# Attention weights transposed on VectorE and moved by DMA between partition quarters, in place of TensorE transposes

## The chip, the cores and the metric

The kernel runs on one core of a Trainium2 chip. The metric is the device time of one execution in microseconds (us). The engines are named as the profile names them: PE (matrix multiplication, with PEld for its weight loads), DVE (vector), ACT (scalar and activation), POOL, and SP, which here only issues DMAs. Each engine works through its own queue of instructions in order, and they meet through semaphores.

## The reference

A batch of 8 matrices x of 512 x 512 (f32) passes four stages, each as `x = x + layernorm(stage(layernorm(x)))`:

```
attention 0:  scores = x^T x;  softmax;  context = weights . x
ffn 0:        x . (sum of 8 factors) / sqrt(8) + bias
attention 1:  RMS norm, 8 query heads and 2 key/value heads of 64,
              softmax(q k^T / 8) v, output projection, + x
ffn 1:        silu(x gate^T * gs) * (x up^T * us), then down^T * ds
```

The change is in attention 1. For each of 8 heads and 512 rows there is a softmax row of 512 weights, and the product with the values needs those weights transposed: the key position must lie on the partitions.

## The kernel before

The whole program is recorded first and ordered afterwards. Class `Recorder` (line 54) takes operations by `add` with an engine, an assumed duration and the buffers that they read and write; `issue` (line 116) then lays them out with a list scheduler: on each engine it takes, among the operations that could start within the engine's `SLACK` of the first, the one with the earliest due time. Due times come from `due` (line 1351) and the tables `DUE` and `SHIFT`; `change` (line 60) is an assumed price of switching the matrix array's shape. The result is a fixed order for each engine in which operations of several batch elements are interleaved. Buffers come from pools: 8 tiles "big" of 128 x 2048, 4 tiles "e" of 128 x 512, 5 and 3 PSUM banks "f" and "g". All loads but the gate, up and down weights are issued on SP, in the order of the list, as are the stores of the output; those weights are loaded from POOL.

`stage_attn1` (line 767) computes for each batch element the transposed normalized input hT, keys kT, values v, and queries qT for four pairs of heads (the two heads of a pair sit in partitions 0-63 and 64-127 and use different key/value heads). `attend(i, u)` (line 934) is the unit of work: head pair i, row half u (256 rows), so 8 units per batch element and 64 in all. For each of its two blocks s of 128 rows:

- line 944 computes the scores of both heads into two PSUM banks;
- `softmax_row` (line 567), for each head: DVE takes the negated maximum (573), ACT the exponential with its sum (580), DVE the reciprocal (590) and DVE scales the row (597);
- line 975 transposes the scaled rows on PE, 16 pieces of 64 x 128, into two PSUM banks;
- line 987 copies them on ACT, two copies, into aT, a tile "big".

Then `values_of` (line 1006) multiplies values with aT, eight matmuls for the unit, and line 1019 copies the result over the queries in qT. `project` (line 1027) is the output projection. For the last batch element (`EARLY`) the units are ordered by row half, and ffn 1 begins on the first half; the other elements go by head pair.

At the first batch element the kernel also sums the factors (line 419) and checks the weights' low bits (line 463), both with DVE work. `layers` is written twice: the second copy runs only if that check fails, and doesn't run here; counts below are of the copy that runs.

Of the kernel before, what the change touches and what calls it, by code (L numbers as in the profile page):

```python
# [17 lines left out]
P = 128  # L18
# [35 lines left out]
class Recorder:  # L54
# [4 lines left out]
    @staticmethod  # L59
    def change(eng, old, new):  # L60


        if new is None or new == old:
            return 0.0
        if eng == "ACT":
            return 1.3
        return 0.09 * (old is None or old.strip("r") != new.strip("r")) + 0.12 * new.endswith("r")

    def __init__(self):
        self.ops = []  # L70
# [178 lines left out]
def layers(  # L249
# [28 lines left out]
    G = 2  # L278
# [285 lines left out]
    def mm(bank, us, go, reads, room=(), state="128x128"):  # L564
        return add("PE", us, go, reads=reads, writes=[bank], room=room, state=state)

    def softmax_row(sc, e):

        nmax, tot, rtot = Buf("s1"), Buf("s1"), Buf("s1")
        add(  # L570
            "DVE",
            0.68,
            lambda: nc.vector.tensor_reduce(nmax.t[:, :], sc.t[:, :], AX.X, ALU.max, negate=True),  # L573
            reads=[sc],
            writes=[nmax],
        )
        add(
            "ACT",
            0.88,
            lambda: nc.scalar.activation(  # L580
                e.t[:, :], sc.t[:, :], AF.Exp, bias=nmax.t[:, :], accum_out=tot.t[:, :]
            ),
            reads=[sc, nmax],
            writes=[e, tot],
            state="exp",
        )
        add(
            "DVE",
            0.16,
            lambda: nc.vector.reciprocal(rtot.t[:, :], tot.t[:, :]),  # L590
            reads=[tot],
            writes=[rtot],
        )
        add(
            "DVE",
            0.48,
            lambda: nc.vector.tensor_scalar(e.t[:, :], e.t[:, :], rtot.t[:, :], None, ALU.mult),  # L597
            reads=[rtot],
            writes=[e],
        )  # L600

    def transpose_to(dst, src, copy="ACT", room=()):

# [20 lines left out]
    def transpose_two(b, t, srcs, room=(), copy=True):  # L624

        pts = [Buf("f") for _ in range(2)]

        def go():  # L630
            for j, r in enumerate(srcs):
                for c in range(KT):
                    for hf in range(2):
                        hp = ts(hf, DH)
                        nc.tensor.transpose(  # L635
                            pts[hf].t[:, :].rearrange("p (j c q) -> p j c q", j=2, c=KT)[:, j, c, :],
                            ap(r)[hp, ts(c, P)],
                            ident[hp, hp],
                        )

        add(
            "PE",
            0.56,
            go,
            reads=[ref(r) for r in srcs],
            writes=pts,
            room=[b, *room],
            state="64x128",
        )

        def into(hf):
            return lambda tt: tt[:, :, t * P : (t + 2) * P].rearrange(
                "p c (j h q) -> p h j c q", j=2, h=2
            )[:, hf, :, :, :]

        def bank(hf):
            return pts[hf].t[:, :].rearrange("p (j c q) -> p j c q", j=2, c=KT)

        if copy:
            for hf in range(2):  # L660

                def go(hf=hf):
                    nc.scalar.copy(into(hf)(b.t), bank(hf))

                add("ACT", 0.6, go, reads=[pts[hf]], writes=[(b, (t, hf)), (b, (t + 1, hf))])
        return pts, into, bank

    def column(b, t):

# [97 lines left out]
    def stage_attn1(x, b):  # L767
# [163 lines left out]

        def attend(i, u):
            aT = Buf("big")
            for s in (2 * u, 2 * u + 1):
                when(kinds[0], b, i, u, s % 2)
                es = [Buf("e") for _ in range(G)]
                scs = [Buf("f") for _ in range(G)]

                def scores(i=i, s=s, scs=scs):
                    for g in range(G):
                        gp = ts(g, DH)
                        nc.tensor.matmul(  # L944
                            scs[g].t[:, :],
                            qT.t[gp, i, ts(s, P)],
                            kT.t[gp, :],
                            start=True,
                            stop=True,
                        )  # L950

                add(
                    "PE",
                    0.87,
                    scores,
                    reads=[(qT, (i, u)), kT],
                    writes=scs,
                    room=[*es, aT],
                    state="64x128",
                )  # L960
                for g in range(G):
                    softmax_row(scs[g], es[g])


                pts = [Buf("f") for _ in range(2)]

                def halves(b):
                    return b.t[:, :].rearrange("p (c q) -> p c q", q=DH)

                def transposes(es=es, pts=pts):  # L970
                    for g in range(G):
                        for t in range(NT):
                            for hf in range(2):
                                hp = ts(hf, DH)
                                nc.tensor.transpose(  # L975
                                    halves(pts[hf])[:, g * NT + t, :],
                                    es[g].t[hp, ts(t, P)],
                                    ident[hp, hp],
                                )

                add("PE", 0.56, transposes, reads=es, writes=pts, room=[aT], state="64x128")
                for hf in range(2):

                    def place(hf=hf, s=s, aT=aT, pts=pts):
                        lo = s % 2 * P + hf * DH
                        copy = nc.scalar.copy
                        copy(columns_of(aT)[:, :, lo : lo + DH], halves(pts[hf]))  # L987

                    add(
                        "ACT",  # L990
                        0.6,
                        place,
                        reads=[pts[hf]],
                        writes=[(aT, 2 * s + hf)],
                    )
            when(kinds[1], b, i, u)
            po = Buf("f")

            def columns_of(b):
                return flat(b.t).rearrange("p (c q) -> p c q", q=2 * P)  # L1000

            def values_of(aT=aT, po=po):
                for t in range(NT):
                    for g in range(G):
                        gp = ts(g, DH)
                        nc.tensor.matmul(  # L1006
                            po.t[gp, : 2 * P],
                            v.t[:, t * P + g * DH : t * P + (g + 1) * DH],
                            columns_of(aT)[:, g * NT + t, :],
                            start=(t == 0),  # L1010
                            stop=(t == NT - 1),
                        )
# [4 lines left out]
                "ACT",  # L1017
                0.4,
                lambda i=i, u=u, po=po: nc.scalar.copy(
                    qT.t[:, i, ts(u, 2 * P)], po.t[:, : 2 * P]  # L1020
                ),
                reads=[po],
                writes=[(qT, (i, u))],
# [264 lines left out]


DUE = {  # L1290
    "x": (-2.595,),
    "fsum": (0.4631, 0.0036),
    "scales": (-1.7557,),
    "wd": (0.2919,),
    "low": (0.8154, 1.1722),
    "a0.norm": (0.602,),
    "a0.row": (-0.0133, 0.0064),
    "a0.out": (0.6155, 0.0012),
    "f0": (-0.2291, 0.103),
    "a1.norm": (0.498, -0.0333),  # L1300
    "a1.kv": (-2.1194,),
    "a1.q": (0.5487, 0.0684),
    "a1.row": (0.5193, 0.0805, 0.0215, -0.0006),
    "a1.mix": (1.3287, 0.0052, 0.0124),
    "a1.out": (1.6207, -0.0361),
    "e1.row": (0.4681, -0.0113, 0.0525, -0.0529),
    "e1.mix": (-2.4837, 58.3341, 0.0746),
    "e1.out": (1.1439, 0.155, 0.0456),
    "f1.norm": (-0.1878, 0.009),
    "f1.gate": (1.5586, 0.0013),  # L1310
    "f1.down": (1.7415, 0.1322, 0.0313),
    "h1.norm": (1.5393, -1.0876, 0.0495),
    "h1.gate": (2.1757, 0.4491, 4.54),
    "h1.down": (1.6071, -1.5421, 1.3412),
}

SHIFT = {
    ("a0", 0): 0.0119,
    ("a1", 0): -0.3641,
    ("f0", 0): 0.0009,  # L1320
    ("f1", 0): -0.1337,
    ("x", 0): 0.0116,
    ("a0", 1): 0.0009,
    ("a1", 1): -0.1282,
    ("f0", 1): -0.3583,
    ("f1", 1): -0.001,
    ("x", 1): 0.0094,
    ("a0", 2): 0.0721,
    ("f1", 2): -0.0021,
    ("x", 2): 0.3533,  # L1330
    ("a1", -2): -0.0219,
    ("f0", -2): -0.0106,
    ("f1", -2): -0.0418,
    ("x", -2): -0.0328,
    ("a0", -1): 0.0045,
    ("a1", -1): -0.1019,
    ("f0", -1): 0.0436,
    ("f1", -1): 0.0947,
}

STAY = {"PE": 0.1755}

SLACK = {"PE": 0.123, "ACT": 0.0985, "DVE": 0.0676, "POOL": 0.7848, "SP": 0.1357}

SMALL = 0.8265
FSUM_POOL = (0, 3)
EARLY = (-1,)
FEW = 4
# [54 lines left out]
```

## Time and profile before

| | |
|---|---|
| median of 3 runs | 1516.56 us (1516.08 to 1517.06) |
| the profiled execution: its own time | 1518.21 us |
| the profiled execution: span from first to last instruction | 1516.3 us |
| granted PE clock | 0.996 |
| DMA traffic | 108.04 MB |
| SP queue (q1): bytes, share of 16 engines | 55.34 MB, 11.5% |

A row of the list of groups reads: line, engine, operation, output <- inputs, shapes, count | busy us, mean ns of one | idle time before, and what ended it. Instructions on PE overlap, so count times mean exceeds busy. An f32 matmul appears as two records, an f32r matmul or a transpose as one. A row of the timeline reads: start, duration, engine, line, and how many like instructions were merged (x16). In a table by stages the columns are the stretch, its length, busy us and count of PE, PEld, DVE, ACT and POOL, the granted clock, the share of the DMA engines and GB/s.

Some rows that the text needs, from the groups with their shapes kept apart:

```profile
L944 PE MATMUL f<-kv,big 64*128 64x512 f32 x512 | 131.2, 613 | 0.1
...
L1099 ACT CAST hl<-hd 128x768 fp32r<-128x768 f32 x32 | 26.7, 836 | 26.0 <-PE g L1233 25.8
...
L1099 ACT CAST hl<-hd 128x640 fp32r<-128x640 f32 x32 | 23.3, 729 | 16.5 <-PE g L1233 9.9 <-DVE hd L1204 6.4
```

### The profile page before, as it was taken

What the parts mean: (1) busy time and instruction counts of PE and PEld (TensorE: products, weight loads), DVE (VectorE), ACT (ScalarE), POOL (GpSimd) and SP (SyncE); (2) the same over time, 40 slices, a digit from 0 to 9 for tenths busy, and PEclk for the clock granted to TensorE, in tenths of its full rate; (3) what the DMA queues carried; (4) which work ended last, traced back from release to release, by engine and by line L of the source; (5) the groups of instructions that cost most, each with busy time, mean ns of one, the idle gap of its engine ahead of it and who ended that gap; (6) DMA issues with size and microseconds to landing.
All of it is one profiled execution on the core that took longest, in us unless ns stands there. A gap on an engine that the chain in (4) does not pass through costs nothing.

```text
span 1516.3 us, 23151 instructions
## 1 busy us (share of the span) xinstructions
PE 1472.7 (97%) x8562; PEld 909.2 (60%) x8562; DVE 1052.4 (69%) x2227; ACT 671.1 (44%) x1426; POOL 578.6 (38%) x884
## 2 busy tenths in 40 slices
PE   5999999999999999999999999999999999999997
PEld 3444557655766557665566656665566655666575
DVE  6899865768558685586846868466774757748745
ACT  3226645642276414663256622565325642266312
POOL 6661142236412374033721347103571116602341
PEclk9999999999999999999999999999999999999999
DMA  9523046112521214212151122411233103420281
GB/s 335 158 84 112 2 105 112 36 42 49 98 63 43 48 44 91 56 48 65 29 104 36 57 56 49 97 37 43 56 70 84 36 15 77 77 63 22 56 161 38
DMA packets 156698, 108.04 MB, mean 71 GB/s; under 512 B 7072, under 2 KB 137120, under 8 KB 156576
## 3 DMA queue, kind: packets, MB, share of 16 engines
q0 software_dynamic: 98736, 51.13, 17.9%
q1 hardware_dynamic: 57840, 55.34, 11.5%
q8 instruction: 70, 1.15, 0.3%
q14 instruction: 52, 0.43, 0.1%
HBM read 98.06 MB, written 8.39 MB: 70 GB/s over the span
## 4 chain that ended last, share of the span: by engine, by line
PE 80%; DVE 9%; POOL 6%; DMA 2%; issue 2%; SPq 0%; ACT 0%; POOLq 0%; DVEq 0%; ACTq 0%
PE g L1165 18%; PE g L1233 11%; PE f L944 7%; PE f L1006 7%; PE f L915 7%; PE f L1032 6%; PE f L724 6%; PE f L975 5%; PE f L693 4%; PE f L746 3%; PE f L635 2%; POOL rstd L532 2%; PE f L896 2%; PE f L885 2%; DVE row L540 1%
## 5 line engine op out<-in xcount | busy, mean ns | idle before, releaser
L1165 PE MATMUL g<-hl,wgu 128*128 128x512 f32 (+1 forms) x1408 | 339.3, 394 | 1.9 <-DMA wgu<-in_gate_t 1.7
L1165 PEld LDWEIGHTS g<-hl,wgu 128*128 128x128 f32 x1408 | 256.7, 189 | 71.9 <-DVE s L573 10.6
L525 POOL TENSOR_SCALAR ve<-mv 128x1 f32<-128x1 f32 x224 | 62.5, 280 | 591.6 <-DVE mv L521 584.4
L573 DVE TENSOR_REDUCE s<-f 128x1 f32<-128x512 f32 x288 | 184.9, 684 | 107.3 <-PE f L944 66.5
L580 ACT ACTIVATE e<-f,s 128x512 f32<-128x512 f32 x288 | 195.9, 688 | 76.5 <-DVE s L573 73.3
L559 POOL TENSOR_TENSOR x<-x,z 128x512 f32<-128x512 f32 x120 | 163.8, 1368 | 48.2 <-DVE z L540 42.7
L1233 PE MATMUL g<-wd,hl 128*128 128x512 f32 x704 | 174.8, 401 | 1.4 <-DVE hl L1108 1.4
L987 ACT COPY big<-f 128x512 f32<-128x512 f32 x256 | 135.9, 593 | 71.8 <-PE f L975 71.5
L1233 PEld LDWEIGHTS g<-wd,hl 128*128 128x128 f32 x704 | 129.4, 188 | 52.3 <-issue 20.7
L597 DVE TENSOR_SCALAR e<-e,s 128x512 f32<-128x512 f32 x288 | 145.3, 508 | 8.4
L532 POOL TENSOR_TENSOR rstd<-ve,mhalf 128x1 f32<-128x1 f32 x224 | 142.0, 638 | 16.0
L387 POOL DMA_DIRECT2D wgu<-in_up_t x92 | 75.0, 815 | 151.1 <-PE g L1165 146.6
L944 PE MATMUL f<-kv,big 64*128 64x512 f32 x512 | 131.2, 613 | 0.1
L1195 DVE SCALAR_TENSOR_TENSOR sig<-g,gs,sig 128x512 f32<-128x512 f32 x84 | 62.7, 747 | 87.4 <-ACT sig L1185 87.1
L1006 PE MATMUL f<-big,kv 128*64 128x256 f32 x1024 | 122.6, 384 | 0.0
L1032 PE MATMUL f<-ws,big 128*128 128x512 f32 x256 | 116.6, 600 | 0.7 <-ACT big L870 0.7
L746 PE MATMUL f<-fsum,rT 128*128 128x512 f32 x256 | 115.7, 595 | 0.2
L915 PE MATMUL f<-big,ws 128*128 128x512 f32 x256 | 115.5, 599 | 0.0
L724 PE MATMUL f<-big,big 128*128 128x512 f32 x256 | 114.8, 597 | 0.0
L1185 ACT ACTIVATE sig<-g,gs 128x512 f32<-128x512 f32 x84 | 58.6, 698 | 119.4 <-PE g L1165 99.6
L387 POOL DMA_DIRECT2D wgu<-in_gate_t x92 | 72.6, 790 | 99.9 <-PE g L1165 93.3
L1204 DVE SCALAR_TENSOR_TENSOR hd<-g,us,sig 128x512 f32<-128x512 f32 x84 | 62.8, 747 | 67.0 <-PE g L1165 63.8
(91 smaller groups left out, 1920.2 us busy)
## 6 DMA issues: line engine op xcount, KB each, us to landing
wgu<-in_gate_t POOLq DMA_DIRECT2D x92, 256.0 KB, 3.3
wgu<-in_up_t POOLq DMA_DIRECT2D x92, 256.0 KB, 3.3
x<-in_x SPq DMA_DIRECT2D x32, 256.0 KB, 2.6
ws<-in_wq_t SPq DMA_DIRECT2D x32, 256.0 KB, 3.3
ws<-in_wo_t SPq DMA_DIRECT2D x32, 256.0 KB, 2.6
out<-x SPq DMA_DIRECT2D x32, 256.0 KB, 2.0
hd<-in_factors SPq DMA_DIRECT2D x28, 256.0 KB, 5.3
wd<-in_down_t POOLq DMA_DIRECT2D x11, 256.0 KB, 8.4
```

The lines of the kernel that those rows point to most:

```text
L532: lambda: nc.gpsimd.tensor_tensor(rstd.t[:, :], ve.t[:, :], mhalf, ALU.pow),
L559: lambda: on.tensor_tensor(ap(xt), ap(xt), y.t[:, :], ALU.add),
L573: lambda: nc.vector.tensor_reduce(nmax.t[:, :], sc.t[:, :], AX.X, ALU.max, negate=True),
L580: lambda: nc.scalar.activation(e.t[:, :], sc.t[:, :], AF.Exp, bias=nmax.t[:, :], accum_out=tot.t[:, :]),
L724: nc.tensor.matmul(po.t[:, :], xnT.t[:, j, ts(t, P)], wT.t[:, j, :], start=(j == 0), stop=(j == KT - 1),)
L746: nc.tensor.matmul(po.t[:, :], xnT.t[:, kt, :], fsum.t[:, kt, :], start=(kt == 0), stop=(kt == KT - 1),)
L915: nc.tensor.matmul(pq.t[:, :], wq.t[:, kt, :], hT.t[:, kt, :], start=(kt == 0), stop=(kt == KT - 1),)
L944: nc.tensor.matmul(scs[g].t[:, :], qT.t[gp, i, ts(s, P)], kT.t[gp, :], start=True, stop=True,)
L1006: nc.tensor.matmul(po.t[gp, : 2 * P], v.t[:, t * P + g * DH : t * P + (g + 1) * DH], columns_of(aT)[:, g * NT + t, :], start=(t == 0), sto ...
L1032: nc.tensor.matmul(po.t[:, :], qT.t[:, i, ts(t, P)], flat(wos[i].t), start=(i == 0), stop=(i == NPAIR - 1),)
L1165: nc.tensor.matmul(bank.t[:, cut], w.t[:, kt, :], d.t[:, kt, cut], start=(n == 0), stop=(n == KT * len(xs) - 1),)
L1233: nc.tensor.matmul(po.t[:, :], ap(o)[:, it - lo, :], wd.t[:, it, :], start=(it == 0 and k == 0), stop=(it == NI - 1 and k == len(ops) - 1),)
```

## The change

In attention 1 the transposes on PE and the copies from PSUM are gone. In their place, for each of the four softmax rows-by-heads of a unit, ACT scales the row by the reciprocal, and DVE transposes it in 32 x 32 blocks into a second tile "big", tb (`small_blocks`). When all four are there, SP issues 16 DMAs of 32 partitions x 512 elements (64 KB) from tb to aT (`to_quarters`): source quarter i goes, in four parts, to the four destination quarters a. The columns of aT come to lie in another order, so the product with the values reads them as four runs of 64, and the copy to qT puts the results back in order. Attention 0 keeps its transposes on PE and its scaling on DVE. The tables of due times, `SHIFT`, `STAY`, `SLACK` and `SMALL` are replaced throughout, and so is the order of instructions on every engine, in all stages.

```diff
-        return 0.09 * (old is None or old.strip("r") != new.strip("r")) + 0.12 * new.endswith("r")
+        if old is not None and old.strip("r") == new.strip("r"):
+            return 0.0
+        return 0.21 if new.endswith("r") else 0.09
...
-    def softmax_row(sc, e):
+    def softmax_row(sc, e, on="DVE"):
...
+        if on == "ACT":
+            add(
+                "ACT",
+                0.6,
+                lambda: nc.scalar.mul(e.t[:, :], e.t[:, :], rtot.t[:, :]),
+                reads=[rtot],
+                writes=[e],
+            )
+        else:
...
+    def small_blocks(dst, n, groups, src, us=0.62):
+        def go():
+            d = flat(dst.t).rearrange(
+                "p (a g k s c) -> p a g k s c", a=4, g=groups, k=KT, c=32
+            )[:, :, n % groups, :, n // groups, :]
+            nc.vector.transpose(d, ap(src).rearrange("p (k a c) -> p a k c", k=KT, a=4))
+
+        add("DVE", us, go, reads=[ref(src)], writes=[(dst, n)])
+
+    def to_quarters(dst, src, us=6.0):
+        def go():
+            for i in range(4):
+                for a in range(4):
+                    nc.sync.dma_start(
+                        flat(dst.t)[ts(a, 32), ts(i, D)], flat(src.t)[ts(i, 32), ts(a, D)]
+                    )
+
+        add("SP", us, go, reads=[src], writes=[dst], lat=2.2)
...
         def attend(i, u):
-            aT = Buf("big")
+            aT, tb = Buf("big"), Buf("big")
...
-                    room=[*es, aT],
+                    room=[*es, tb],
                     state="64x128",
                 )
                 for g in range(G):
-                    softmax_row(scs[g], es[g])
...
-                add("PE", 0.56, transposes, reads=es, writes=pts, room=[aT], state="64x128")
-                for hf in range(2):
...
-                        copy(columns_of(aT)[:, :, lo : lo + DH], halves(pts[hf]))
...
+                    softmax_row(scs[g], es[g], "ACT")
+                    small_blocks(tb, s % 2 * G + g, G, whole(es[g]))
+            to_quarters(aT, tb)
...
-                return flat(b.t).rearrange("p (c q) -> p c q", q=2 * P)
+                return flat(b.t).rearrange("p (i c q) -> p c i q", i=4, q=2 * 32)
...
-                            po.t[gp, : 2 * P],
+                            po.t[gp, : 2 * P].rearrange("p (i q) -> p i q", i=4),
                             v.t[:, t * P + g * DH : t * P + (g + 1) * DH],
-                            columns_of(aT)[:, g * NT + t, :],
+                            columns_of(aT)[:, g * NT + t, :, :],
...
-                    qT.t[:, i, ts(u, 2 * P)], po.t[:, : 2 * P]
+                    qT.t[:, i, ts(u, 2 * P)].rearrange("p (s i c) -> p i s c", s=2, i=4),
+                    po.t[:, : 2 * P].rearrange("p (i s c) -> p i s c", s=2, i=4),
...
-    "a1.row": (0.5193, 0.0805, 0.0215, -0.0006),
-    "a1.mix": (1.3287, 0.0052, 0.0124),
+    "a1.row": (0.6822, 0.0734, 0.1964, -0.0076),
+    "a1.mix": (1.4015, 0.1652, 0.0008),
...
-STAY = {"PE": 0.1755}
-
-SLACK = {"PE": 0.123, "ACT": 0.0985, "DVE": 0.0676, "POOL": 0.7848, "SP": 0.1357}
-
-SMALL = 0.8265
+STAY = {"PE": 0.3655}
+
+SLACK = {"PE": 0.4719, "ACT": 0.3146, "DVE": 0.1972, "POOL": 0.4366, "SP": 0.1357}
+
+SMALL = 1.6694
```

More of the change, by code (lines that the diff above doesn't have):

```diff
@@ L593, in softmax_row @@
         )
[L594 to L600, printed above, removed]
+        if on == "ACT":
[7 more added lines that the diff above has]
+        else:
+            add(
+                "DVE",
+                0.48,
+                lambda: nc.vector.tensor_scalar(e.t[:, :], e.t[:, :], rtot.t[:, :], None, ALU.mult),
+                reads=[rtot],
+                writes=[e],
+            )
     def transpose_to(dst, src, copy="ACT", room=()):
@@ L666, in transpose_two @@
         return pts, into, bank
+    def small_blocks(dst, n, groups, src, us=0.62):
[11 more added lines that the diff above has]
+                        flat(dst.t)[ts(a, 32), ts(i, D)], flat(src.t)[ts(i, 32), ts(a, D)]
+                    )
+        add("SP", us, go, reads=[src], writes=[dst], lat=2.2)
     def column(b, t):
@@ L961, in attend @@
                 for g in range(G):
-                    softmax_row(scs[g], es[g])
[L965 to L972, printed above, removed]
-                            for hf in range(2):
[L974 to L979, printed above, removed]
-                add("PE", 0.56, transposes, reads=es, writes=pts, room=[aT], state="64x128")
[L982 to L995, printed above, removed]
+                    softmax_row(scs[g], es[g], "ACT")
+                    small_blocks(tb, s % 2 * G + g, G, whole(es[g]))
+            to_quarters(aT, tb)
             when(kinds[1], b, i, u)
@@ L1290 @@
 DUE = {
[L1291 to L1302, printed above, removed]
-    "a1.row": (0.5193, 0.0805, 0.0215, -0.0006),
-    "a1.mix": (1.3287, 0.0052, 0.0124),
-    "a1.out": (1.6207, -0.0361),
-    "e1.row": (0.4681, -0.0113, 0.0525, -0.0529),
@@ L1307 @@
[L1307 to L1314, printed above, removed]
+    "x": (-4.5218,),
+    "fsum": (-0.547, 0.014),
+    "scales": (-1.2959,),
+    "wd": (-0.7415,),
+    "low": (1.8698, 0.1987),
+    "a0.norm": (0.0158,),
+    "a0.row": (-0.0659, -0.763),
@@ new lines @@
+    "a0.out": (0.9091, -0.0574),
+    "f0": (-0.3562, 0.1296),
+    "a1.norm": (-0.3362, 0.1194),
+    "a1.kv": (-1.2134,),
+    "a1.q": (0.5561, 0.1876),
+    "a1.row": (0.6822, 0.0734, 0.1964, -0.0076),
+    "a1.mix": (1.4015, 0.1652, 0.0008),
+    "a1.out": (2.1241, -0.0582),
+    "e1.row": (0.1817, 0.0337, 0.8262, -0.0122),
+    "e1.mix": (-3.788, 317450.7115, 0.0865),
+    "e1.out": (2.4047, 0.0474, -0.0519),
+    "f1.norm": (-0.6898, 0.8102),
+    "f1.gate": (1.1806, 0.0018),
+    "f1.down": (1.9561, 0.2922, 0.0028),
@@ L1315 @@
+    "h1.norm": (1.4106, -0.7397, 1.6211),
+    "h1.gate": (3.3436, 0.0244, 0.1058),
+    "h1.down": (0.7682, -266.647, 0.0299),
 }
 SHIFT = {
[L1318 to L1338, printed above, removed]
-}
-STAY = {"PE": 0.1755}
-SLACK = {"PE": 0.123, "ACT": 0.0985, "DVE": 0.0676, "POOL": 0.7848, "SP": 0.1357}
-SMALL = 0.8265
+    ("a0", 0): -0.1698,
+    ("a1", 0): -0.2727,
+    ("f0", 0): -0.235,
+    ("f1", 0): 0.2207,
+    ("x", 0): 0.5279,
+    ("a0", 1): 0.1932,
+    ("f0", 1): 0.2686,
+    ("x", 1): 0.1051,
+    ("a0", 2): 0.1267,
+    ("a1", 2): -0.1561,
@@ L1346 @@
+    ("f1", 2): -0.003,
+    ("x", 2): 0.0002,
+    ("a0", -2): 0.0203,
+    ("f0", -2): 0.0665,
+    ("f1", -2): 0.0816,
+    ("x", -2): 0.1179,
+    ("a0", -1): 0.5856,
+    ("a1", -1): -0.4355,
+    ("f0", -1): -0.3224,
+    ("f1", -1): -0.0373,
+}
+STAY = {"PE": 0.3655}
+SLACK = {"PE": 0.4719, "ACT": 0.3146, "DVE": 0.1972, "POOL": 0.4366, "SP": 0.1357}
+SMALL = 1.6694
 FSUM_POOL = (0, 3)
```

## The prediction

> **What bounds the kernel now.** I read the page's busy times first, then its chain, then the groups of PE with their shapes kept apart.
>
> ```profile
> PE 1472.7 (97%) x8562; PEld 909.2 (60%) x8562; DVE 1052.4 (69%) x2227; ACT 671.1 (44%) x1426; POOL 578.6 (38%) x884
> ...
> PE 80%; DVE 9%; POOL 6%; DMA 2%; issue 2%; SPq 0%; ACT 0%; POOLq 0%; DVEq 0%; ACTq 0%
> ```
>
> ```profile
> L1006 PE MATMUL f<-big,kv 128*64 128x256 f32 x1024 | 122.6, 384 | 0.0
> ...
> L975 PE MATMUL f<-ident,e 64*128 64x64 f32 x2048 | 88.0, 228 | 0.5 <-ACT big L987 0.4
> ```
>
> PE is the bound: 43.6 us of 1516.3 idle, and 80% of the chain. L975, the group that goes, holds 88.0 us of PE and hardly waits. The second number of a row (228 ns) is one instruction's life; they overlap, so it can't be multiplied. Next, what a set of 16 costs from its start to the next group's start, in PE's timeline (start, duration):
>
> ```profile
> 1400.88 0.71 PE L975 MATMUL f<-ident,e 64*128 64x64 f32 x16
> 1401.52 3.67 PE L1006 MATMUL f<-big,kv 128*64 128x256 f32 x32
> 1405.13 0.71 PE L975 MATMUL f<-ident,e 64*128 64x64 f32 x16
> 1405.68 1.96 PE L944 MATMUL f<-kv,big 64*128 64x512 f32 x8
> ```
>
> 0.64 and 0.55 us here; over the whole timeline 77.7 us for 128 sets. The chain of waits gives L975 4.8%, 73 us. Then the stages, with the busy time of PE, PEld, DVE, ACT and POOL in each, and the groups on other engines that the change touches.
>
> ```profile
> 80.00:120.00 40.00, 38.91 (x160) 19.24 (x160) 37.15 (x78) 11.19 (x31) 21.52 (x34) 1.00 0.41 125
> 120.00:160.00 40.00, 39.47 (x282) 19.54 (x281) 35.85 (x87) 23.39 (x57) 9.99 (x17) 1.00 0.17 54
> ...
> 400.00:600.00 200.00, 198.94 (x1150) 122.94 (x1149) 128.78 (x276) 88.44 (x190) 72.17 (x110) 1.00 0.27 61
> ```
>
> ```profile
> L573 DVE TENSOR_REDUCE s<-f 128x1 f32<-128x512 f32 x288 | 184.9, 684 | 107.3 <-PE f L944 66.5
> ...
> L987 ACT COPY big<-f 128x512 f32<-128x512 f32 x256 | 135.9, 593 | 71.8 <-PE f L975 71.5
> ...
> L597 DVE TENSOR_SCALAR e<-e,s 128x512 f32<-128x512 f32 x288 | 145.3, 508 | 8.4
> ```
>
> From 80 to 160 us DVE is 91% busy, nearly as tight as PE; in the middle of the kernel it has 36% free. Last, SP's timeline at the start and the page's DMA issues:
>
> ```profile
> 0.73 1.81 SPq L366 DMA_DIRECT2D x<-in_x  x4
> ```
>
> ```profile
> out<-x SPq DMA_DIRECT2D x32, 256.0 KB, 2.0
> ```
>
> Four issues in 1.81 us are 0.45 us each; the shortest landing on the page is 2.0 us.
>
> **What the Trainium skill says.** "DMA: Bandwidth & Descriptors", "Anatomy of one DMA — SWDGE (gpsimd) path": a transfer has a fixed cost of about 2 us, mostly the receipt. The 2.0 us above agrees, though from another queue and with 256 KB. "VectorE: DVE Perf Modes", "The three transpose paths": DVE transposes only within 32x32 blocks (so quarters must still be exchanged), 311 ns for 128x128 bf16. No trace here shows this operation. "Vector Engine (DVE) Microarchitecture Reference", section 3.8: it sustains one element per cycle per lane. "VectorE: DVE Perf Modes", the errata section: one-element-per-cycle operations cost (N+151)/0.96 ns, 691 ns at 512; the trace's reductions agree (684).
>
> **The change, part by part.**
>
> 1. *PE.* 2048 transposes go (the built order shows none left, and the other counts of PE unchanged): -77.7 us by start-to-start; bounds -73 (chain) and -88 (busy). Values (L1006) now read four runs of 64 columns in place of 256; still 256 columns, so I take 0, bounds 0 to +12 (a tenth of 122.6). If nothing else ended later: span 1516.3 - 77.7 = 1438.6.
>
> 2. *ACT.* 256 copies of 593 ns go (-152), 256 scalings from SBUF come. L1099 has such operations with 640 and 768 elements, 729 and 836 ns; continued to 512 that is 622 ns, +159. Net +7 us on an engine 44% busy: beside other work. But the scaling now stands between reciprocal and transpose.
>
> 3. *DVE.* 256 scalings of 508 ns go (-130); 256 block transposes come. I take 0.70 us (one element per cycle, as the reductions); low end 0.60, high end 1.2 (four bytes at half the rate). Net +49 (+24 to +177): DVE about 1100 of 1440 us, 76%. Hidden by PE in the middle, not from 80 to 160 us.
>
> 4. *SP and DMA.* 64 times 16 transfers of 64 KB. Issue 16 x 0.45 = 7.2 us (bounds 0.38, the shortest single issue seen, and 0.86, the spacing of two weight loads in SP's timeline at 712 us), landing 2.0 us after the last (bounds 1.5 and 4). In the built order each waits for the transfer eight before it: 8 x 0.45 = 3.6 us later, so a 2 us landing doesn't hold it up, a 4 us landing would. The first waits for the fourth block transpose; behind it on SP lie weight loads, x loads and output stores. In all 1024 x 0.45 = 461 us on a queue that has 1440. Traffic 67 MB more; 55.34 MB took 11.5% of the engines, so about 14% more beside some 30%: room.
>
> 5. *The new wait.* Values wait for all 16 landings, and everything behind waits on PE with them. Cost of the step: DVE's work from the last two rows' reductions to the last transpose (summed along DVE's built order for each of the 64 units, median 6.1 us at the prices above, times 1052/1124, the page's union against the sum of rows), plus 7.2 + 2.0, plus 0.4 for handing over: 15.3 us in the median. Cover: PE work between a unit's last scores and its values in the built order, at start-to-start prices. An example: 64 gate/up matmuls 15.6 us, 6 scores 2.9, 8 values 1.9: 20.4 us. Over 64 units the median is 19 us, the lowest 8.7. I summed cover minus step over the units for several lengths of the step. With a median step of 14.7 us, 8 units fall short, 18 us in sum, 14 of it in the first batch; 1 us longer 28 us, 2 us longer 40, 4 us longer 84, 6 us longer 148. To the 15.3 us I add 1.5 us for queueing on ACT between exponential and scaling, which the sum along DVE leaves out: 2.1 us longer, 42 us. These sums are upper bounds, since two or three units are in flight and one stall lengthens the cover of the next: I take half, 21 us. The first batch alone supports 11 of that: its eight values stand 43 us apart in PE work, while DVE needs 60 us of listed work x 0.94 = 56 between them and SP seven exchanges of 7.2 us, 50.
>
> 6. *Rewritten order* (due times, slack). The order is built from these tables for every stage, so gaps shift at the start (about 18 us wait for the first x) and the end (loads of gate and up weights at 1440-1458). I take +2, bounds -6 and +12.
>
> 7. *Pools.* A unit now holds two big tiles from its scores to its landing (aT and tb) in place of one; the first transpose into a reused tb waits on DVE for earlier transfers, and reductions of other rows lie behind it. This is inside point 5's half; without cover it would cost DVE a landing, 2 us, per unit at worst.
>
> Sum: 1516.3 - 77.7 + 21 + 2 = 1461.6. The profiled execution took 1518.21 us with a span of 1516.3; the median of the runs shown is 1516.56, practically the span. So I take 1462.
>
> **The rivals.**
> - *All hidden.* The transfers fit in the cover. For it: median cover 19 us, DVE and SP far from full. Against: the first batch. 1438.6 + 2 = about 1440.
> - *DVE bound.* Transposes at 1.2 us: four of them lengthen a step by 2 us, to 4.1 above the 14.7 (shortfalls 87, half 43), and DVE grows to 1230 us, 85%; in the first batch, where it binds, 32 x 0.5 = 16 us more, of which I count half. 1438.6 + 43 + 8 = about 1490.
> - *Slower: the exchange of quarters outlasts the cover.* Place: PE before the values. A landing of 4 us holds up the second eight transfers too (about +3 us), an issue of 0.7 us costs +4, an SP that stands at a store until POOL is done (such waits sum to 204 us in SP's waits now) with an exchange behind it costs several more. If stalls didn't overlap it would decide 3.7 us above the 14.7 (shortfalls 78); with half, at about 6.2. At 8 us above, the shortfalls are 236, half 118: 1438.6 + 118 = about 1557. Against it: SP waits are idle time on a queue with little to do now, and 2.0 us was seen for four times the bytes.
> - *The change doesn't do what it says*: excluded, the built order has the transposes gone.
>
> **How the numbers follow.** Forecast (1450 to 1478) 0.42; all hidden 0.25; DVE bound or a step some 4 us longer (1478 to 1513) 0.17; slower 0.13; about the same 0.03. About 0.2%, 3 us, is what a measurement of this kernel can tell from no change. Leaving out the slowest case and the edge of the quick one, the range is 1437 to 1505. Faster 0.84, same 0.03, slower 0.13.
>
> **What would show it.** Right: PE busy near 1395, no f<-ident,e group besides attention 0's; a StreamTranspose row near 0.70 us; ACT scaling near 0.62; SP issues 0.45 apart and landings near 2 us; PE waits before the values' line of some 20 us in sum, mostly before 200 us. Wrong: landings of 4 us, PE waits before values above 80 us, values dearer than 120 ns each, DVE above 85%.

## The result, and the profile after

The changed kernel takes 1590.54 us (median of 4 runs, 1584.93 to 1593.11) where the kernel before took 1516.81 (4 runs, 1516.08 to 1518.6): ratio 1.0479, 95% interval 1.0466 to 1.0491. The forecast was 1462, the range 1437 to 1505. The profiled execution took 1591.39 us with a span of 1589.6.

Busy times and the chain of the kernel after:

```profile
PE 1441.8 (91%) x6514; PEld 858.2 (54%) x6514; DVE 1106.0 (70%) x2227; ACT 707.2 (44%) x1436; POOL 568.3 (36%) x884
...
PE 55%; DVE 13%; SPq 12%; POOL 6%; DMA 6%; issue 4%; ACT 3%; POOLq 0%; DVEq 0%; ACTq 0%
```

The 2048 transposes are gone from PE's count (8562 to 6514), and yet PE's busy time falls by 31 us only. SP's queue, 0% of the chain before, has 12% of it. The groups that the change touches, and the DMA row:

```profile
L1011 PE MATMUL f<-big,kv 128*64 128x256 f32 x1024 | 146.0, 435 | 82.9 <-DMA big<-big 80.1
L689 DVE STREAM_TRANSPOSE big<-e 128x512 f32<-128x512 f32 x256 | 172.1, 699 | 42.0 <-ACT e L601 38.4
...
L601 ACT ACTIVATE e<-e,s 128x512 f32<-128x512 f32 x256 | 174.9, 718 | 36.1 <-DVE s L593 35.1
...
big<-big SPq DMA_DIRECT2D x1024, 64.0 KB, 2.0
```

The block transpose (0.699 us) and the landing (2.0 us) are what the forecast took. The values' row is not: PE stands 80.1 us before it for the exchange, and the matmuls themselves hold 146.0 us where they held 122.6. So two things are to be explained, a wait and a slowness.

*The wait.* First the duration of single issues on SP (min/median/max ns), in the kernel before for a load from HBM, then in the kernel after for the exchange:

```profile
L366 SPq DMA_DIRECT2D x<-in_x x32: 327/328/973, 0.7 to 1203.0; - x32
```

```profile
L697 SPq DMA_DIRECT2D big<-big x1024: 507/588/1890, 121.2 to 1492.0; - x171
```

And SP's timeline in the first batch element (start, duration, how many merged):

```profile
121.23 10.10 SPq L697 DMA_DIRECT2D big<-big  x16
...
133.02 10.92 SPq L697 DMA_DIRECT2D big<-big  x16
...
144.67 62.92 SPq L697 DMA_DIRECT2D big<-big  x96
```

An exchange keeps SP for 10.0 us or more (0.626 an issue), not 7.2, and six follow one another without a gap at 10.5 us each: here SP sets the pace. PE's timeline shows that pace and the slowness beside it (the bracket is the idle time before a set and what ended it):

```profile
156.57 1.95 PE L1011 MATMUL f<-big,kv 128*64 128x256 f32 x16 [2.82 <-DMA big<-big]
158.44 1.99 PE L980 MATMUL f<-kv,big 64*128 64x512 f32 x8
166.88 3.68 PE L1011 MATMUL f<-big,kv 128*64 128x256 f32 x16 [6.45 <-DMA big<-big]
170.49 1.94 PE L980 MATMUL f<-kv,big 64*128 64x512 f32 x4
172.26 0.76 PE L647 MATMUL f<-ident,big 64*128 64x64 f32 x16
178.10 3.68 PE L1011 MATMUL f<-big,kv 128*64 128x256 f32 x16 [5.08 <-DMA big<-big]
```

Values come every 10.3 to 11.2 us here, and from one to the next PE's fixed order has work for only 4 to 6 us, the values themselves included.

*The slowness.* A set is the product of one unit with the values, eight matmuls and so 16 records. The set after a wait of 2.82 us takes 1.95 us, as it does without a wait; the sets after 6.45 and 5.08 us take 3.68. In the whole timeline of this kernel all 31 sets of 16 without a wait take 1.95, those after a wait of 4.0 us or more take 3.3 to 3.7, those after less than 2.4 take 1.95, and between these limits both occur. What follows at once is slow as well: four records of the scores take 1.94 us where eight take 1.99. The trace has the granted clock beside it (a table by stages; the clock is the third number from the end):

```profile
165.30:172.10 6.80, 5.22 (x20) 2.63 (x21) 0.48 (x1) 1.50 (x4) 0.00 (x0) 0.50 0.44 104
182.40:199.50 17.10, 12.22 (x48) 5.16 (x46) 14.38 (x34) 9.03 (x21) 7.09 (x10) 1.00 0.41 98
```

It is at half in the stretch with the set at 166.88, and full in the stretch with a set at 188.63 that had no wait and took 1.95. The Trainium skill, "TensorE: Matmul & The Clock Gate", section "What's actually happening", describes such a clock: after a window of about 3.4 us without work PE falls to half its clock, and needs about 3.4 us of sustained work to come back; the window runs freely, so the same wait can fall on either side. The trace agrees in kind (a clock of 0.50, and both outcomes for waits of 2.4 to 4.0 us). In size it differs: four sets are slow after waits of 2.55 to 2.77 us, shorter than that window. The core's line (span, granted clock), before and after:

```profile
core 0: 1516.3 us, clock 0.996
```

```profile
core 0: 1589.6 us, clock 0.968
```

0.4% of 1516 are 6 us, 3.2% of 1590 are 51: 45 us more lost to the clock. Counted another way: the transposes held 76.5 us of PE's busy time before (from each set's start to the next start, without gaps), so PE's other work took 1472.7 - 76.5 = 1396.2 us, and takes 1441.8 after. That is 45.6 us more, of which values 23.1, scores 9.8, keys and queries 4.8.

The whole account: 1516.3 - 76.5 (the transposes) + 45.6 (slower matmuls) + 104.2 (PE idle 147.8 us in place of 43.6, 80.1 of it before values) = 1589.6.

### The profile page after: what moved, and what is told of

The parts are those of the page before. It is cut to its first block, busy times and chain, and to the rows that moved or that the text cites. A ratio compares the mean times of both kernels' runs of the same rounds, so it can differ in the third digit from the quotient of the medians.

```text
span 1589.6 us, 20499 instructions
## 1 busy us (share of the span) xinstructions
PE 1441.8 (91%) x6514; PEld 858.2 (54%) x6514; DVE 1106.0 (70%) x2227; ACT 707.2 (44%) x1436; POOL 568.3 (36%) x884
## 4 chain that ended last, share of the span: by engine, by line
PE 55%; DVE 13%; SPq 12%; POOL 6%; DMA 6%; issue 4%; ACT 3%; POOLq 0%; DVEq 0%; ACTq 0%
PE g L1171 14%; SPq L697 12%; PE g L1239 8%; PE f L1011 6%; PE f L980 5%; PE f L950 5%; PE f L759 4%; PE f L1038 4%; PE f L781 3%; DMA big<-big 3%; DVE st L518 2%; PE f L920 2%; POOL rstd L534 2%; PE f L728 2%; PE f L931 2%
## 5 line engine op out<-in xcount | busy, mean ns | idle before, releaser
L1171 PE MATMUL g<-hl,wgu 128*128 128x512 f32 (+1 forms) x1408 | 331.7, 391 | 3.6 <-DMA wgu<-in_gate_t 1.8
L527 POOL TENSOR_SCALAR ve<-mv 128x1 f32<-128x1 f32 x224 | 68.1, 304 | 568.7 <-DVE mv L523 544.7
L1011 PE MATMUL f<-big,kv 128*64 128x256 f32 x1024 | 146.0, 435 | 82.9 <-DMA big<-big 80.1
L689 DVE STREAM_TRANSPOSE big<-e 128x512 f32<-128x512 f32 x256 | 172.1, 699 | 42.0 <-ACT e L601 38.4
L601 ACT ACTIVATE e<-e,s 128x512 f32<-128x512 f32 x256 | 174.9, 718 | 36.1 <-DVE s L593 35.1
L1239 PE MATMUL g<-wd,hl 128*128 128x512 f32 x704 | 180.9, 408 | 2.4 <-DVE hl L1114 2.3
L1011 PEld LDWEIGHTS f<-big,kv 128*64 128x64 f32 x1024 | 83.7, 154 | 150.8 <-issue 102.8
L980 PE MATMUL f<-kv,big 64*128 64x512 f32 x512 | 141.9, 638 | 0.1
L534 POOL TENSOR_TENSOR rstd<-ve,mhalf 128x1 f32<-128x1 f32 x224 | 133.1, 596 | 15.7
L759 PE MATMUL f<-big,big 128*128 128x512 f32 x256 | 120.5, 619 | 7.8 <-ACT e L583 4.8
```

The lines of the kernel that those rows point to most:

```text
L601: lambda: nc.scalar.mul(e.t[:, :], e.t[:, :], rtot.t[:, :]),
L689: nc.vector.transpose(d, ap(src).rearrange("p (k a c) -> p a k c", k=KT, a=4))
L759: nc.tensor.matmul(po.t[:, :], xnT.t[:, j, ts(t, P)], wT.t[:, j, :], start=(j == 0), stop=(j == KT - 1),)
L980: nc.tensor.matmul(scs[g].t[:, :], qT.t[gp, i, ts(s, P)], kT.t[gp, :], start=True, stop=True,)
L1011: nc.tensor.matmul(po.t[gp, : 2 * P].rearrange("p (i q) -> p i q", i=4), v.t[:, t * P + g * DH : t * P + (g + 1) * DH], columns_of(aT)[:, ...
L1171: nc.tensor.matmul(bank.t[:, cut], w.t[:, kt, :], d.t[:, kt, cut], start=(n == 0), stop=(n == KT * len(xs) - 1),)
```

## The experiments

The theory after reading the trace ("issue"): the 16 issues with both ends in SBUF take 0.6 us each, so the step from the last block transpose to the values is 12.0 us in place of 9.2, exchanges of several units queue on SP, PE waits, and after long waits runs slow. Rivals: "bytes", the 67 MB more of traffic or the landing hold it up; "order", the new tables and the order laid from them cost the time. Each run was timed beside the kernel before on the same chip; the ratios are to that.

**Four transfers for sixteen.** Same bytes, same order; the quarters come to lie in wrong places.

```diff
-                for a in range(4):
-                    nc.sync.dma_start(
-                        flat(dst.t)[ts(a, 32), ts(i, D)], flat(src.t)[ts(i, 32), ts(a, D)]
-                    )
+                nc.sync.dma_start(flat(dst.t)[ts((i + 1) % 4, 32), :], flat(src.t)[ts(i, 32), :])
```

> The exchange as 4 transfers of 256 KB (a whole source quarter of 32 partitions to the next quarter) in place of 16 of 64 KB: the same bytes, and the order of all instructions as in the changed kernel. The blocks don't reach the places that the product with the values needs, so the weights are in the wrong places. Theory (issue): the 16 issues of 0.63 us are what is late; 4 take about 2.5 us, PE's wait before the values falls from 83 us to under 15, the clock goes back to above 0.985, and the kernel takes 1440 to 1470 us. Rival (bytes): the 67 MB between partitions and their landing under load are what is late; PE still waits 60 us or more there and the kernel takes over 1555. Rival (order): the rewritten tables are what costs; over 1555 too.

1492.55 us, ratio 0.983 (0.9806 to 0.9855). Single issues last as long as before for four times the bytes:

```profile
L696 SPq DMA_DIRECT2D big<-big x256: 507/590/2257, 122.3 to 1389.5; - x128
```

PE no longer waits for the exchange, although a landing takes 4.4 us. 98 us come back with fewer issues of the same bytes: "bytes" falls. The order of all instructions is that of the changed kernel, and the time lies below the kernel before: "order" by itself can't be what made the change slower. The expectation of 1440 to 1470 was missed all the same, by 22 us; see the run with eight.

**Every second transfer issued from ACT.** Eight issues on each queue, the exchange complete.

```diff
-                    nc.sync.dma_start(
+                    on = nc.scalar if (4 * i + a) % 2 == 1 else nc.sync
+                    on.dma_start(
```

> Every second of the 16 transfers is issued from ACT in place of SP, at the same point of the recorded order; nothing else changes and the result is complete. Theory (issue): the exchange takes half as long (about 5 us plus landing), PE's wait before the values falls below 30 us; ACT gets 512 issues of some 0.6 us, about 307 us more of its time, in which exponentials stand behind them. 1470 to 1540 us. Rival (bytes): the same bytes at the same time, so 1575 to 1605. Rival (order): 1575 to 1605.

1790.61 us, ratio 1.1799 (1.1778 to 1.182). The expectation missed by 250 us. An issue takes ACT's queue as long as SP's, 602 ns in the median and 309 us for all 512, and the queue is in order. The expectation had this sum and supposed that ACT could bear it. The profile lists the time as waits for the exchange (engine, tile, line, what ended the wait: us in all, times, longest):

```profile
ACT L1192 <- DMA big<-big: 124.8, 18, 8.5
ACT e L583 <- DMA big<-big: 117.8, 20, 8.2
```

ACT's timeline shows what fills such a wait:

```profile
258.19 5.29 ACTq L698 DMA_DIRECT2D big<-big  x8
263.53 0.72 ACT L601 ACTIVATE e<-e,s 128x512 f32<-128x512 f32 x1 [5.23 <-DMA big<-big]
```

These are ACT's own eight issues, which don't count as busy time. In the same way some 178 of the 242.6 us ahead of the sigmoids (1192) and exponentials (583) are issues, and PE stands behind these. So the run agrees with "issue" on the price of a transfer, from another queue; and a queue with other duties is no place for an exchange.

**The kernel before with the scaling on ACT alone,** the order laid anew from the tables of before.

```diff
...
-                    softmax_row(scs[g], es[g])
+                    softmax_row(scs[g], es[g], "ACT")
```

> The kernel before with only one part of the change: the rows of the second attention are scaled on ACT in place of DVE, the transposes stay on PE; tables as before, the list is laid out anew with this operation. Theory (issue): this part costs little, 1510 to 1535 us. Rival (chain of softmax): the longer way between exponential and transpose over ACT is a main part of the loss; above 1545.

1654.08 us, ratio 1.0903 (1.0885 to 1.0921): again far worse than expected, and by the number what the rival named (above 1545). Here ACT scales and copies from PSUM too; in the changed kernel the copies are gone. Its chain:

```profile
PE 68%; ACT 15%; DVE 7%; POOL 4%; DMA 3%; issue 2%; SPq 0%; POOLq 0%; DVEq 0%; ACTq 0%
```

ACT has 15% of the chain where it had 0% in the kernel before and has 3% in the changed one. The kernels with four and eight transfers scale on ACT as the changed one does and take 1492, so the scaling isn't what made the change slower. What it costs in them by itself was not measured. The order's tables weren't fitted to this kernel either; how much of the 1654 that is stays open.

**The kernel before with the new price of switching shapes alone.** The expectation speaks of all tables of the change. The kernel that ran has only one part of them, the new body of `change` (line 60); its due times, `SHIFT`, `STAY`, `SLACK` and `SMALL` are those of before.

> The kernel before with only the tables of the change (due times, shift, stay, slack, small, and the price of switching the array). Theory (issue): 1505 to 1545 us, since tables tuned for other work fit this one less well. Rival (order): the new order is itself the loss; above 1570.

1513.57 us (8 runs), ratio 0.9975 (0.9964 to 0.9986): slightly faster. So this price costs nothing by itself. It says nothing of the other tables: no run had them with the operations of before. Where a later expectation speaks of the new order alone, it means this kernel.

**Eight transfers for sixteen,** to see whether the time follows the number of issues; wrong places again.

```diff
-                for a in range(4):
+                for h in range(2):
...
-                        flat(dst.t)[ts(a, 32), ts(i, D)], flat(src.t)[ts(i, 32), ts(a, D)]
+                        flat(dst.t)[ts((i + 1) % 4, 32), ts(h, 2 * D)],
+                        flat(src.t)[ts(i, 32), ts(h, 2 * D)],
```

> The exchange as 8 transfers of 128 KB (half of a source quarter's row each, to the next quarter); same bytes and order as in the changed kernel, the blocks in the wrong places. Theory (issue): 8 x 0.63 = 5.0 us plus some 3 us of landing, between the four (6.9 us, 1492 us) and the sixteen (12.0 us, 1590 us): 1492 to 1515 us, PE's wait on the transfers before the values under 10 us. Rival (bytes): the loss goes with the number of transfers only by chance; above 1540.

1492.22 us, ratio 0.9845 (0.9829 to 0.9861), the same as with four. At some 5 us of issue the exchange is covered but for 1.1 us; what is left on PE is other waits:

```profile
L1012 PE MATMUL f<-big,kv 128*64 128x256 f32 x1024 | 126.8, 392 | 5.0 <-ACT e L583 2.2 <-ACT e L601 1.4 <-DMA big<-big 1.1
...
L647 PE MATMUL f<-ident,row 64*128 64x64 f32 x512 | 23.2, 229 | 11.9 <-DVE row L542 11.0 <-DVE mv L523 0.9
```

The values are back at 126.8 us (122.6 before). So a kernel with the forecast's gain and hardly a wait for the exchange is at 1492 with this order, not at 1440 as the rival "all hidden" had it: PE is idle for 74.9 us, against 43.6 before, and its work takes 1414.6 us, against the 1396.2 of the kernel before without its transposes.

**Fifteen of the sixteen transfers read HBM.** Same number, same size, same destinations; the values are multiplied with input rows in place of most of the weights. This puts the forecast's issue price into the changed kernel.

```diff
+                    far = x_in[a, ts(4 * i + a, 32), :]
...
-                        flat(dst.t)[ts(a, 32), ts(i, D)], flat(src.t)[ts(i, 32), ts(a, D)]
+                        flat(dst.t)[ts(a, 32), ts(i, D)],
+                        flat(src.t)[ts(i, 32), ts(a, D)] if i == a == 0 else far,
```

> 16 transfers of 64 KB into the same destinations, but only the first reads the transposed tile; the other 15 read 32 rows of x from HBM. Weights are replaced by other numbers. It asks whether an issue is long because both ends lie in SBUF. If so: an issue of about 0.38 to 0.45 us as for the loads, the exchange takes 16 x 0.42 + 2.5 = 9.2 us as the prediction assumed, and the kernel takes 1490 to 1525 us. If an issue is long because of 32 partitions in place of 128: 0.6 us and 1575 to 1610 us.

1511.47 us (6 runs), ratio 0.9966 (0.9953 to 0.9978). The two kinds of issue side by side on one queue, and PE's wait for the exchange:

```profile
L698 SPq DMA_DIRECT2D big<-in_x x960: 310/419/1946, 123.1 to 1410.0; - x192
...
L698 SPq DMA_DIRECT2D big<-big x64: 512/513/607, 122.4 to 1402.7; - x64
```

```profile
PE f L1013 <- DMA big<-in_x: 16.2, 8, 3.3
```

Only the source differs, and the time falls by 79 us. (That tb comes free sooner is not the reason: DVE's block transposes wait 2.2 us for transfers here and 2.4 in the changed kernel.) At about the forecast's price (15 issues in 7.2 us in the median) PE waits 16.2 us for the exchange; the forecast had 21. That part of the sum holds, and still the kernel is not at 1462.

**Sixteen transfers over all 128 partitions,** SBUF to SBUF, 128 columns each, nothing exchanged: is it the narrow 32 partitions or the two ends?

```diff
-                    nc.sync.dma_start(
-                        flat(dst.t)[ts(a, 32), ts(i, D)], flat(src.t)[ts(i, 32), ts(a, D)]
-                    )
+                    at = slice((4 * i + a) * P, (4 * i + a + 1) * P)
+                    nc.sync.dma_start(flat(dst.t)[:, at], flat(src.t)[:, at])
```

> 16 transfers of 64 KB from the transposed tile to the other, each over all 128 partitions with 128 columns (nothing changes its partition, so the weights are in the wrong places). Both ends in SBUF, but 128 partitions. If both ends in SBUF make the issue long: about 0.6 us and 1575 to 1620 us. If 32 partitions do: about 0.4 us and 1490 to 1525 us.

1557.98 us, ratio 1.027 (1.0253 to 1.0287), between the two expectations.

```profile
L698 SPq DMA_DIRECT2D big<-big x1024: 464/599/2043, 121.0 to 1461.2; - x171
```

```profile
144.56 63.20 SPq L698 DMA_DIRECT2D big<-big  x96
```

```profile
164.69 0.62 PE L1010 MATMUL f<-big,kv 128*64 128x256 f32 x2 [3.80 <-DMA big<-big]
165.88 3.45 PE L1010 MATMUL f<-big,kv 128*64 128x256 f32 x14 [0.57 <-DMA big<-big]
...
175.01 4.86 PE L1010 MATMUL f<-big,kv 128*64 128x256 f32 x16 [3.22 <-DMA big<-big]
```

The issue stays at 0.6 us with 128 partitions, and six exchanges take 63 us as in the changed kernel (62.92): it goes with both ends in SBUF, not with the narrow tile. PE starts earlier for another reason: here each transfer brings whole columns, so a set of values begins with its first matmul (two records) while the rest is still on its way. PE's waits at the line sum to 38.5 us, and more of its waiting lies inside the sets, as 4.86 us for one of them shows; the values still come some 10 us apart.

**The changed kernel with an order laid from the measured prices.** All operations as they are; the exchange is planned at 10.2 us of SP, the transpose at 0.68, the scaling at 0.7, and due times and slacks are searched anew.

```diff
-                0.6,
+                0.7,
...
-    def small_blocks(dst, n, groups, src, us=0.62):
+    def small_blocks(dst, n, groups, src, us=0.68):
...
-    def to_quarters(dst, src, us=6.0):
+    def to_quarters(dst, src, us=10.2):
```

> The changed kernel with all its operations and transfers as they are; only the prices from which the order is laid are the measured ones (the exchange 10.2 us on SP where the change has 6.0, the block transpose 0.68, the scaling on ACT 0.7), and the due times and slacks are searched anew for them. Theory issue: an exchange occupies SP for 10 us and lands 2 us later whatever the order, so a knowing order can spread the units but not shorten the step; it wins back a part of the 74 us: 1540 to 1590, PE still waiting at the values for 30 us or more, or waiting as long elsewhere. Rival, only the plan was wrong: with a right price in the plan the step is covered, PE waits under 15 us before the values, and the time is that of the run with eight transfers or near it, below 1505.

1544.78 us, ratio 1.0184 (1.0166 to 1.0202). A better order halves PE's wait and can't remove it:

```profile
PE f L1012 <- DMA big<-big: 41.5, 15, 9.7
```

So an order laid for the measured prices takes back 46 of the 74 us; the other 28 stay in the best one that this search found.

**The exchange through HBM,** complete: the transposed blocks are stored in one transfer and loaded back in four, and the order is searched anew.

```diff
-                        flat(dst.t)[ts(a, 32), ts(i, D)], flat(src.t)[ts(i, 32), ts(a, D)]
+            nc.sync.dma_start(hop.t[:, :], flat(src.t))
...
+            for a in range(4):
+                nc.sync.dma_start(
+                    flat(dst.t)[ts(a, 32), :].rearrange("r (i c) -> r i c", i=4),
+                    hop.t[:, ts(a, D)].rearrange("(i r) c -> r i c", i=4),
+                )
```

> The changed kernel with the exchange of quarters in another form and complete: the transposed blocks go to a tile in HBM in one store of 256 KB, and four loads of 64 KB bring the quarters back, each to 32 partitions. Five issues with one end in HBM in place of sixteen with both ends in SBUF; the order is searched anew for it. Theory issue: at 0.33 to 0.42 us an issue the exchange occupies SP for about 2 us, but two landings follow one another, some 2.2 and 2.5 to 4 us, so a step of 7 to 9 us after the last block transpose where the changed kernel has 12; bursts of units are no longer held to 10.5 us each. Expected 1480 to 1510, waits before the values under 25 us. Rival, bytes and landings decide (each landing after the first costs its 2 to 4 us on PE, HBM traffic grows by 34 MB): the step is no shorter, 1530 or more. If it lies below 1513.6 it beats both kernels and the one with the new order alone.

1675.22 us, ratio 1.1031 (1.1013 to 1.1048): a clear miss, and the rival's mechanism. The expectation had the sizes wrong by a factor of four: a unit is 1 MB, so the store has 1024 KB and each load 256, and the traffic grew by 67 MB over that of the changed kernel. DMA rows (KB each, us to landing) and SP's timeline:

```profile
hop<-big SPq DMA_DIRECT2D x64, 1024.0 KB, 5.1
big<-hop SPq DMA_DIRECT2D x256, 256.0 KB, 5.5
```

```profile
145.68 0.33 SPq L699 DMA_DIRECT2D hop<-big  x1
149.52 1.75 SPq L703 DMA_DIRECT2D big<-hop  x4
156.50 0.34 SPq L699 DMA_DIRECT2D hop<-big  x1
160.42 1.73 SPq L703 DMA_DIRECT2D big<-hop  x4
```

The issues are as short as expected (0.33, and four in 1.75), but the loads wait for the store's landing, so at the median landings the step is 0.3 + 5.1 + 1.7 + 5.5 = 12.6 us, no shorter than the 12.0 of the changed kernel, and SP stands at each store with everything behind it. PE waits 140.4 us before the values, at a clock of 0.948.

**Twelve transfers for sixteen,** complete: the four blocks that stay in their quarter are copied on POOL, and the order is searched anew.

```diff
+                    if a != i:
                         nc.sync.dma_start(
                             flat(dst.t)[ts(a, 32), ts(i, D)], flat(src.t)[ts(i, 32), ts(a, D)]
                         )
+        def stay(a):
+            nc.gpsimd.tensor_copy(flat(dst.t)[ts(a, 32), ts(a, D)], flat(src.t)[ts(a, 32), ts(a, D)])
```

> The changed kernel, complete, with twelve transfers for sixteen: the four blocks whose quarter stays the same are copied on POOL (32 x 512 each) and the other twelve are moved by DMA as before; the order is searched anew with 7.7 us for the exchange and 0.7 for a copy. Theory issue: 12 x 0.626 = 7.5 us on SP and 2.0 us of landing, about the step that the forecast had (9.2), with both ends of every transfer in SBUF and no part left out. Against the run with the new order and sixteen transfers (1544.8) the step is 2.5 us shorter; the run with fifteen transfers from HBM had about this step and took 1511. Expected 1490 to 1520, PE waiting under 25 us for the exchange, clock 0.98 or better. Rival, copies on another engine bring a new wait: POOL's queue stands at weight loads until PE is done with a buffer, the copies lie behind them, and PE waits for POOL before the values instead: 1530 or more, with that wait named by the profile. Below 1513.6 it would beat every complete kernel so far.

1516.96 us (21 runs, 1512.04 to 1520.62), ratio 0.9997 (0.9989 to 1.0005): within the expectation, and equal to the kernel before. SP's timeline, and PE's wait:

```profile
124.29 7.55 SPq L698 DMA_DIRECT2D big<-big  x12
...
133.40 54.65 SPq L698 DMA_DIRECT2D big<-big  x84
```

```profile
PE f L1017 <- DMA big<-big: 10.8, 4, 4.2
```

Seven exchanges in 54.65 us are 7.8 each; the kernel takes 28 us less than with sixteen transfers (each with an order of its own), and PE's wait falls from 41.5 to 10.8. PE hardly waits for the copies on POOL (0.607 us each; 8.6 us of wait at the weight loads), so the rival falls. This is about the forecast's step in a complete kernel, and it gives 1517, not 1462: PE idles 85.9 us of 1510.4 (43.6 before), of which 10.8 for the exchange, and the clock of 0.981 loses 29 us (6 before). No complete kernel here is faster than the one before with the new price of switching shapes (1513.57).

## Why the prediction was wrong, step by step

The sum was 1516.3 - 77.7 + 21 + 2 = 1461.6, against a span of 1589.6.

1. *Transposes on PE, -77.7:* right. They are gone; without the gaps they held 76.5. The values' new reading order costs nothing: a set without a wait takes 1.95 us, as before. Values did grow dearer than the 120 ns each that the prediction named as a sign of being wrong (146.0 us for 1024 records, 143 ns), but by the clock.
2. *ACT:* the scaling took 718 ns where 622 was drawn from wider casts, 25 us more in all. ACT has 3% of the chain, where it had none, and DVE stands 38.4 us ahead of the block transposes for the scaling: mostly beside other work, not wholly.
3. *DVE:* right, 699 ns against 0.70; DVE at 70%. The rival "DVE bound" is out.
4. *Issue and landing:* the step that failed first. "Issue 16 x 0.45 = 7.2 us" took the price from loads out of HBM. With both ends in SBUF an issue costs 0.626 us, inside the bounds (0.38 to 0.86), so 10.0 us; the landing is the 2.0 us it was put at. The count was right; the row that its price came from was another kind of transfer. (The lower bound was misread: the shortest single issue in that trace is 0.327 us, as the row of L366 shows, not 0.38.) The Trainium skill, "DMA: Bandwidth & Descriptors", section "Issuing engines are not separate DMA queues", calls the time to initiate a DMA usually small relative to the DMA itself. Here one issue is nearly a third of a landing (0.63 of 2.0 us), and sixteen in a row are 10.0 us ahead of the last landing, so the measurement decides against it for this step. The prediction also named the loads that stand behind the exchange on SP and gave them no price: DVE waits 33.4 us for rows of x in the changed kernel, 8.4 before and 11.0 with eight transfers.
5. *The wait, +21:* it is 80.1. 2.8 us on the step bring it to 4.9 us above the 14.7, where the forecast's own shortfalls (84 at 4, 148 at 6) give about 113. Taking half of them gives 56; the run shows 0.71 of them. The halving supposed that stalls lengthen the next unit's cover. Where SP goes from one exchange straight into the next, they don't: the next unit's transfers are late by as much (read from the timeline; no run tests the factor). In the first batch element the eight values stand 76.1 us apart, 133.15 to 209.23 (forecast: 43 of PE, 56 of DVE, 50 of SP), with 24 us of waits for the exchange; forecast 11. The other 56 lie later, where the forecast had 10. With about the issue price of the forecast the wait is 16.2 us (the run with fifteen from HBM) where it had 21: this term was mis-sized by the price in the first place, and at the longer step by the half. The 80.1 is also just above the 80 us that the prediction had named as a sign of being wrong.
6. *Order, +2 (-6 to +12):* wrong. Against before, PE's idle time that doesn't wait for the exchange grew by 104.2 - 80.1 = 24 us in the changed kernel, and by 30.5 with four transfers. With eight the largest are 11.0 at the transposes of normalized rows (1.6 before) and 7.8 at the product of attention 0 with its weights (none before). The two orders with tables searched anew for the direct exchange (sixteen and twelve transfers) have as much of it, 74 and 75 us against 68 in the changed kernel and 43.6 before, so it doesn't hang on one set of tables; most likely it comes with the new operations on DVE and ACT. No run separates the two, since none had the tables of the change with the operations of before.
7. *What was in no step:* PE at half speed after long waits, 46 us. The forecast took a stall to cost its own length and put this at nothing. Even with four or eight transfers the clock is 0.987, 13 us more lost than before.

Added up: +59 at the wait, +46 at the clock, +22 in other gaps, +1 at the transposes, 1462 + 128 = 1590. The run with fifteen transfers from HBM splits it differently: 79 of the 128 us go with the issue price, in waits and in slow matmuls. The other 49 would have been missed with the right price as well, and twelve transfers in a complete kernel say the same (55 above the forecast).

The rival "slower: the exchange of quarters outlasts the cover" had the place and the sign right and named an issue of 0.7 us as one way to it. It was put at 0.13 because it needed 6.2 us above the 14.7 to decide; it decided at 4.9, since waits weren't halved as a whole and long ones are paid for again at half the clock.

The relation of wait and clock over the runs (PE's wait for the exchange, us, and granted clock): before 0 and 0.996; four transfers 0, 0.987; eight 1.1, 0.987; twelve 10.8, 0.981; fifteen from HBM 16.2, 0.984; sixteen over 128 partitions 38.5, 0.978; new order 41.5, 0.976; changed 80.1, 0.968; through HBM 140.4, 0.948. It falls with the waits but for one pair (twelve and fifteen); other long waits count too, as the first runs show. That it is the waits which set the clock down is read from the timelines, and agrees with the page named above; a kernel with the same waits filled by other work on PE was not tried.

## What to carry to other kernels

Price a DMA issue from a row with the same two ends: on this queue a transfer inside SBUF took 0.59 us in the median and a load from HBM 0.33 to 0.42, whatever the size from 64 to 256 KB, so count the transfers, not the bytes. When work that comes in bursts is handed to a queue, ask for the rate of the queue in the burst (here 10.5 us a unit against some 6 of PE work), not for its share of the whole span. And count a long PE stall at more than its length: from 4.0 us on, every set behind one ran slow here, and below that some did.

## What the runs showed of the hardware

- An issue on SP: 0.31 us at best and 0.42 in the median from HBM to 32 partitions, 0.33 in the median for x from HBM to 128 partitions (before), 0.46 to 0.51 at best and 0.59 to 0.60 in the median from SBUF to SBUF, the same for 64, 128 and 256 KB and for 32 and 128 partitions. A store to HBM took 0.34 in the median, of 256 KB (before) as of 1 MB. From ACT's queue an issue from SBUF to SBUF took 0.51 at best and 0.60 in the median.
- In the changed kernel, sets of values after a PE wait of 4.0 us or more ran at about half speed (3.3 to 3.7 us in place of 1.95), and none after a wait below 2.4 us did. In other runs some did after shorter waits (1.91 us with the exchange through HBM). In a slow stretch the granted clock was 0.50.
- Landings from SBUF to SBUF: 2.0 us for 64 KB, 2.4 for 128, 4.4 for 256; a store of 1 MB to HBM 5.1, and 256 KB from there to 32 partitions 5.5.
